# A graph network on one core: attention 1 over fixed tiles of the edge list, 24 of 49 destination blocks dense

## The chip, the cores and the metric

One core of a Trainium2 chip runs the whole program. The metric is the device time of one execution in microseconds; the time before is the median of three runs, 4275.56 us (4267.46 to 4278.62).

The core has engines that run side by side, each its own instructions in order, and that wait for one another by semaphores: PE (matmuls, into the accumulator memory PSUM), DVE (VectorE), ACT (ScalarE), POOL (GpSimd, which here gathers rows by index) and SP (which here issues transfers). DMA queues move data between DRAM and the on-chip memory (SBUF).

## The reference

A graph of 6250 nodes and 200,000 edges, sorted by destination. Two layers of graph attention, then an edge convolution, each behind a layer norm and a relu, each added to x:

```
h = relu(layernorm(x))
x = x + attention2(elu(attention1(h)))        # attention 1: 4 heads of 16; attention 2: 1 head of 128
h = relu(layernorm(x))
x = x + convolution(h, edge attributes)

attention(x):
    feat = x @ W                              # per node
    el, er = sum(feat * attn_l), sum(feat * attn_r)
    e = leaky_relu(el[src] + er[dst], 0.2)    # per edge
    alpha = softmax of e over the edges of each dst
    out[dst] = sum of feat[src] * alpha + bias
```

## The kernel before

Nodes lie in 49 blocks of 128 (the last has 106). The program has four stages.

**Prelude.** x is loaded (`load_x`), normalised, and multiplied by the weights in groups of four blocks (`features`, five steps pipelined by `through`). `write_table` writes a row of 76 floats per node to the DRAM tensor table1: features, logit, and exp(el) and exp(0.2 el). Beside that the sorted edge list is searched: `segments`, `fetch_parts`, `count_parts` and `window_rows` find where each pair of nodes starts (for the counts), `block_segments` and `block_firsts` where each block of 128 nodes starts. Most of these instructions are wrapped in `keep`, which holds an engine's instructions in the written order; the rest is ordered by the framework's scheduler.

**Attention 1** treats its blocks in one of two ways, interleaved in one loop.

*Gathered blocks* (29, in order): a block's edges lie in a window of 34 x 128 = 4352 list entries (CAP), loaded by `load_window` from a start read at run time. Per block, GROUPS cuts the 34 columns in four groups of eight and one of two. For each column `gather` issues one indirect DMA (L346) that fetches 128 table rows by source index into a tile G (six buffers). `attend` then builds a one-hot matrix of the destinations (`ohr`, L351), spreads the destination factors to the edges by matmuls (L387) with the mask `oht` (L377, from a row broadcast to all partitions by `load_low`, L371), takes the larger of the two weights (L389 to L393), multiplies (L394), splits the messages in two halves (L358 on ACT, L359 on DVE), and scatters by one matmul per column (L404) into one accumulator `whole`. At a block's end `sums` are read out (L1038 on ACT, L1039 on DVE), and every four blocks `finish1` ends them.

*Dense blocks* (the last 20, DENSE1): `dense1` works with counts instead of edges: the number of edges between every pair of nodes. One pass treats four destination blocks and two heads and runs over the 49 source blocks seven at a time. It loads the counts `ctc` (L911, 16 transfers of 56 KB each time) and right-hand rows `rc` (L914), builds a steep ramp on ACT (`up`, L942, seven per step), takes its minimum with the counts on DVE (L945), and multiplies on PE (L952, L958). A pass is 16 steps: one that starts it, 14, one that ends it (L965 to L993). Five groups of four blocks and two pairs of heads make ten passes.

*The counts* of all 49 blocks are made in the same loop, in quarters of a block (`cut_windows`, then `count`: one-hots on DVE, L823; matmuls, L834; copies on ACT, L836; a write of 392 KB, L838). Attention 2 reads all of them.

The loop runs over gathered groups. After each, `due` says how many of the 196 counting steps and of the 160 dense steps must have been started: counting ends AFTER = 3 blocks (102 tiles) before the last group, dense steps begin after LAG_D = 3 blocks and end AFTER_D = 20 tiles before the last. `step` delays part of each step by one, so that engines overlap. `fill_rhs1` makes the right-hand rows in the first seven groups.

**Handover.** After the loop the windows of the remaining blocks are loaded too, though no gather reads them, flags are computed, and one run-time test asks whether a general fallback must run (L503). Then the memory of attention 1 is given back.

**Attention 2** runs over pairs of blocks with all counts (`ct`, L1209, eight transfers of 392 KB per pair), the logits spread by L1211 and L1214, ramps on ACT (L1228), minima on DVE (L1232, L1233) and matmuls (L1237). x is loaded again at the second pair. Then the **convolution** over all edges with 1563 gathers.

Memory is handed out by pools; a pool opened after another was closed may lie in its memory, and then waits until that is free. G's pool `gath` of attention 1 is opened after the prelude's pools are closed.

```
GROUPS = ((0, 8), (8, 8), (16, 8), (24, 8), (32, 2))
K = 34
CAP = P * K
AHEAD = 4
DENSE1, LAG_D, AFTER, AFTER_D = 20, 3, 3, 20
```

Of the kernel before, what the change touches and what calls it, by code (L numbers as in the profile page):

```python
# [30 lines left out]
F32 = mybir.dt.float32  # L31
# [13 lines left out]
GROUPS = ((0, 8), (8, 8), (16, 8), (24, 8), (32, 2))  # L45
K = 34
CAP = P * K
# [6 lines left out]
AHEAD = 4  # L54
DENSE1, LAG_D, AFTER, AFTER_D = 20, 3, 3, 20
# [10 lines left out]
def gnn_kernel(ctx: ExitStack, tc: tile.TileContext, x, src, dst, attr4, attr8,  # L66
               W1, al1, ar1, b1, W2, al2, ar2, b2,
               Wl0, Wl1, Ws0, Ws1, Wm1, Wm2, Wtp, Wf0, Wf1, src_t, dst_t, attr4_t, attr8_t, runs,
# [12 lines left out]
    assert NCHUNK * GP * GK == E and E >= CAP and E % (GP * SEG) == 0  # L81
# [13 lines left out]
    NT = src_t.shape[1]  # L95
    NCH = -(-NT // CT)
# [7 lines left out]
    ps_sm = ps_one.enter_context(tc.tile_pool(name="ps_sm", bufs=2, space=PSUM))  # L104
    ps_pre = ExitStack()
# [43 lines left out]
    def load_x():  # L149
        nc.vector.memset(xt[:, FULL, :], 0.0)  # L150
        for b in range(0, FULL, 8):
            n = min(8, FULL - b)
            (nc.scalar, nc.sync)[b // 8 % 2].dma_start(
                xt[:, b:b + n, :], x[b * P:(b + n) * P, :].rearrange("(b p) f -> p b f", p=P))
        nc.scalar.dma_start(xt[:REST, FULL, :], x[FULL * P:, :])
# [5 lines left out]
    pool = one.enter_context(tc.tile_pool(name="att1", bufs=1))  # L161
    seek = ExitStack()
# [6 lines left out]
    nc.sync.dma_start(di[:, :ROWT], rows)  # L169
    nc.sync.dma_start(di[:GP - 1, ROWT:], rows[1:, :1])  # L170
# [8 lines left out]
    w1_sb = const.tile([D, HD], F32, name="w1_sb")  # L179
    nc.scalar.dma_start(w1_sb, W1)  # L180
    a1_sb = const.tile([HD, 2 * H1], F32, name="a1_sb")
    nc.scalar.dma_start(a1_sb, a1_w)
    load_x()

    first_i = const.tile([1, NB], I32, name="first_i")
    over = const.tile([1, NB], F32, name="over")
# [16 lines left out]
    def segments(i0, i1):  # L203
        for i in range(i0, i1):
            below = find.tile([GP, NC * P], BF16, name="belowc", bufs=2)
            keep(nc.vector.tensor_scalar(below, wstarts, df[:, i * WSEG:i * WSEG + 1], None, op0=OP.is_gt))
            for c in range(NC):
                keep(nc.tensor.matmul(pcount[:, c:c + 1], below[:, c * P:(c + 1) * P], ones_b, start=i + c == 0,
                                      stop=i == NSEG - 1 and c == NC - 1))
# [36 lines left out]
    def block_segments():  # L246
        below = find.tile([GP, NB + 1, NS], F32, name="below")
# [12 lines left out]
    def block_firsts():  # L260
# [9 lines left out]
        first = find.tile([1, NB], F32, name="first")  # L270
        keep(nc.vector.tensor_scalar(first, ends[:, :NB], float(E - CAP), None, op0=OP.min))
        keep(nc.vector.tensor_copy(first_i, first))
        keep(nc.vector.tensor_sub(over, ends[:, 1:], first))
        keep(nc.vector.tensor_scalar(over, over, float(CAP), None, op0=OP.is_gt))
        keep(nc.vector.tensor_sub(n_edges, ends[:, 1:], ends[:, :NB]))

    def find_falls():
        falls = find.tile([GP, ROWT], F32, name="falls")
# [6 lines left out]
        keep(nc.vector.tensor_tensor(over, over, falls_at_all, op=OP.max))  # L285

    def low_parts():
        low_i = find.tile([GP, ROWT], I32, name="low_i")
# [7 lines left out]
    def window_start(b):  # L296
        return nc.values_load(
            first_i[0:1, b:b + 1], engines=[SP], min_val=0, max_val=E - CAP,
            skip_runtime_bounds_check_because="first is clamped to this range where it is computed")


    srcw = pool.tile([P, NB, K], I32, name="srcw")
    dstw = pool.tile([P, NB, K], F32, name="dstw")
    raw_dst = {}

    def load_window(b):
        r = window_start(b)
        nc.sync.dma_start(srcw[:, b, :], src[ds(r, CAP)].rearrange("(p k) -> p k", p=P))
        raw_dst[b] = work.tile([P, K], I32, name="dsti", bufs=AHEAD)
        nc.sync.dma_start(raw_dst[b], dst[ds(r, CAP)].rearrange("(p k) -> p k", p=P))  # L310

    def shift_window(b):
        keep(nc.vector.tensor_scalar(dstw[:, b, :], raw_dst.pop(b), -float(b * P), None, op0=OP.add))
# [55 lines left out]
    def load_low(b):  # L369
        t = aw.tile([P, CAP], BF16, name="oht")  # L370
        nc.sync.dma_start(t, dlow[ds(window_start(b), CAP)].partition_broadcast(P))  # L371
        return t

    def node_hot(t):


        nc.vector.tensor_scalar(t, t, own, None, op0=OP.is_equal)  # L377
        return t.rearrange("n (p k) -> n k p", k=K)

# [166 lines left out]
    def rows_of(table, b0, n):  # L546
# [4 lines left out]
    w1t = transposed([w1_sb], HD, nc.vector.tensor_copy)  # L551
    ps = small()
    nc.tensor.matmul(ps[:D, :2 * H1], w1t[:HD, 0, :], a1_sb, start=True, stop=True)
    nc.vector.tensor_copy(ext1[:, :HD], w1_sb)
    nc.vector.tensor_copy(ext1[:, HD:], ps[:D, :2 * H1])
# [17 lines left out]
    slot_k = pool.tile([P, P, 2], BF16, name="slot_k")  # L573
    nc.gpsimd.iota(slot_k, pattern=[[1, P], [0, 2]], base=0, channel_multiplier=0,
                   allow_small_or_imprecise_dtypes=True)
    slot_b = pool.tile([P, P], BF16, name="slot_b")
    nc.gpsimd.iota(slot_b, pattern=[[1, P]], base=0, channel_multiplier=0,
                   allow_small_or_imprecise_dtypes=True)
    pq3 = pool.tile([P, NB, 2 * H1, 3], BF16, name="pq3")
# [16 lines left out]
    def stats(i):  # L596
        b0, n = 8 * i, 8 if i < NB // 8 - 1 else NB - 8 * i
# [3 lines left out]
        c = coefs(b0, n, mv)  # L601
        next(c)
        return c

    co = {}
    w = HD + 2 * H1
# [41 lines left out]
    c0 = stats(0)  # L648
    keep(nc.vector.tensor_copy(df, di))
    deque(c0, 0)  # L650
    c1 = stats(1)
    through(0)
    segments(0, 1)
    through(1)
    deque(c1, 0)
    segments(1, 5)
    c2 = stats(2)
    through(2)
    through(3)
    segments(5, 6)  # L660
    deque(c2, 0)
    segments(6, NSEG)
    window_segments()
    for q in range(2):
        fetch_parts(q)
    c3 = stats(3)
    through(4)
    through(5)
    block_segments()
    deque(c3, 0)  # L670
    c4 = stats(4)
    through(6)
    through(7)
    block_firsts()
    deque(c4, 0)
    c5 = stats(5)
    through(8)
    count_parts(0)
    fetch_parts(2)
    deque(c5, 0)  # L680
    low_parts()
    through(9)
    write_table(0, 24)
    through(10)
    count_parts(1)
    fetch_parts(3)
    through(11)
    through(12)
    count_parts(2)
    fetch_parts(4)  # L690
    through(13)
    write_table(24, 40)
    through(14)
    through(15)
    through(16)
    write_table(40, NB)
    pq = pool.tile([P, NB, 2 * H1], F32, name="pq")
    node_factors(pq, er1, H1)
    split3(pre, pq3, pq, [P, NB, 2 * H1])
    for q in range(3, 5):  # L700
        count_parts(q)
    window_rows()
    sel1 = pool.tile([P, NB, H1], F32, name="sel1")
    nc.vector.tensor_scalar(sel1, t1[:, :, HD:HD + H1], STEEP, None, op0=OP.mult)
    wide1 = widely(pool, t1[:, :, HD:HD + H1])
    find_falls()
# [339 lines left out]

    for b in range(AHEAD):
        load_window(b)
# [563 lines left out]
```

## Time and profile before

| | us |
|---|---|
| median of three runs | 4275.56 |
| the profiled execution | 4266.29 |
| its span, first to last instruction | 4264.5 |
| first to last gather of attention 1 (L346, table1) | 114.4 to 1656.7 |
| first ramp of attention 2 (L1228) | 1707.0 |
| first gather of the convolution | 2289.6 |
| busy over the span: PE, DVE, ACT, POOL | 3058.5, 3570.7, 2829.5, 2703.0 |

A group in the profile names line, engine, operation and tiles, then shapes and how often it ran, its busy time and the mean duration of one in ns, and the idle time of the engine just before with what ended it ("issue" is time in which the engine waited for nothing that the profile shows). A wait line says who waited for whom, the total, how often, and the longest. A timeline line has start, duration, engine, line, operation, tiles, and in brackets the idle time before it and what ended it. Instructions of one engine may overlap a little in the records, so the sum of groups is above the busy time of the engine.

### The profile page before, as it was taken

The page shows a single profiled execution, that of the slowest core. Times are in us where ns is not written, and L with a number is a line of the kernel's source. Part 1 is how long each engine was busy: PE and PEld are TensorE (multiplying, and loading weights), DVE is VectorE, ACT ScalarE, POOL GpSimd, SP SyncE. Part 2 cuts the span into 40 slices and gives each one's busy share as a digit, 9 for nine tenths or more (in the row PEclk, how much of TensorE's full clock was granted, in tenths as well). Part 3 has the DMA queues.
Part 4 walks back from the last instruction along what each step waited for, and adds up shares of the span by engine and source line. Part 5 has one row for each costly group of instructions (what it writes and reads, how often), then busy time and mean ns, then how long its engine had stood idle before and what let it go on. Part 6 is the DMA issues. An engine that isn't in the chain of part 4 may idle for free. (4 is left out here: it accounts for less than half of the span.)

```text
span 4264.5 us, 62159 instructions
## 1 busy us (share of the span) xinstructions
PE 3058.5 (72%) x19331; PEld 2133.9 (50%) x19332; DVE 3570.7 (84%) x6078; ACT 2829.5 (66%) x6395; POOL 2703.0 (63%) x2616
## 2 busy tenths in 40 slices
PE   3365657667767765799996777777777777777777
PEld 3254444444544543688884444444444444444444
DVE  5887868888888875788886999989999998998988
ACT  3456757777777674799995656555555655555655
POOL 3777777777777774100003777777777777777775
PEclk9997868877777776899997888888888888888888
DMA  3555656656666663644441222222222222222221
GB/s 84 163 173 158 171 146 178 174 163 172 184 168 172 170 164 82 248 162 157 166 147 52 62 64 63 62 63 62 64 62 63 62 63 64 62 63 63 63 61 50
DMA packets 413231, 486.83 MB, mean 114 GB/s; under 512 B 251997, under 2 KB 300187, under 8 KB 409165
## 3 DMA queue, kind: packets, MB, share of 16 engines
q1 hardware_dynamic: 293108, 252.64, 20.5%
q0 software_dynamic: 84000, 146.30, 14.4%
q10 hardware_dynamic: 35768, 83.68, 5.2%
q8 instruction: 160, 2.62, 0.3%
q14 instruction: 195, 1.59, 0.1%
HBM read 378.89 MB, written 103.42 MB: 113 GB/s over the span
## 5 line engine op out<-in xcount | busy, mean ns | idle before, releaser
L346 POOL DMA_INDIRECT G<-table,srcc x1563 | 1474.8, 944 | 1003.3 <-DVE kept L1279 527.2
L346 POOL DMA_INDIRECT G<-table,srcw x986 | 1149.5, 1166 | 362.6 <-issue 269.0
L942 ACT ACTIVATE up<-erb,sel 128x512 bf16<-128x512 f32 x980 | 637.0, 723 | 11.8 <-DMA counts<-ca 5.9
L836 ACT CAST ca<-small 128x392 bf16<-128x392 f32 x784 | 350.0, 490 | 239.8 <-PE small L834 221.8
L1373 PE MATMUL whole<-halves,ohr 128*128 128x512 f32 x1563 | 506.8, 463 | 0.7 <-ACT acc L1403 0.7
L1228 ACT ACTIVATE ramp<-erb,sel 128x256 bf16<-128x256 f32 (+1 forms) x1225 | 491.4, 495 | 21.3 <-DVE up L1232 17.4
L1315 ACT ACTIVATE g<-G,a 128x128 f32<-128x128 f32 x1563 | 481.0, 392 | 1.8 <-DMA G<-table,srcc 0.9
L1308 PEld LDWEIGHTS big<-wtp_sb,hid 64*128 64x128 f32 x3126 | 266.1, 251 | 372.4 <-issue 357.5
L958 PE MATMUL up<-up,rc 128*102 128x512 bf16 x980 | 342.7, 507 | 148.6 <-DVE up L945 148.4
L1308 PE MATMUL big<-wtp_sb,hid 64*128 64x128 f32 x3126 | 309.1, 353 | 151.8 <-DVE halves L1362 151.3
L834 PE MATMUL small<-key,lo 128*128 128x98 bf16 x3136 | 295.4, 233 | 129.8 <-ACT ca L836 97.8
L1373 PEld LDWEIGHTS whole<-halves,ohr 128*128 128x128 f32 x1563 | 317.0, 210 | 132.4 <-issue 58.5
L1299 ACT ACTIVATE hid<-layer 128x512 f32<-128x512 f32 x392 | 230.5, 588 | 191.2 <-PE layer L1296 191.2
L1296 PE MATMUL layer<-hid,wm_sb 128*128 128x512 f32 x392 | 342.7, 972 | 12.5 <-ACT hid L1299 11.8
L1296 PE MATMUL layer<-a8t,wm_sb 16*128 16x512 f32 x392 | 230.7, 669 | 153.0 <-ACT hid L1299 141.9
L945 DVE TENSOR_TENSOR up<-up,ctc 128x3584 bf16<-128x3584 bf16 x140 | 282.8, 2021 | 68.2 <-ACT up L942 56.6
L834 PEld LDWEIGHTS <-lo 128*128 128x128 bf16 x3136 | 227.9, 113 | 211.6 <-issue 157.5
L1353 ACT CAST halves<-mess 128x512 fp32r<-128x512 f32 x195 | 114.3, 586 | 329.7 <-DVE mess L1340 329.7
L1345 DVE TENSOR_TENSOR halves<-mess,halves 128x512 fp32r<-128x512 f32 x391 | 267.8, 685 | 60.5 <-ACT halves L1348 43.6
L823 DVE TENSOR_TENSOR lo<-slots,turned 128x2048 bf16<-128x2048 bf16 x196 | 238.6, 1217 | 63.2 <-PE small L834 62.4
L958 PEld LDWEIGHTS <-rc 128*102 128x102 bf16 x980 | 157.9, 165 | 265.3 <-issue 234.4
L1237 PE MATMUL big<-rhs,up 128*128 128x196 bf16 x2401 | 240.6, 250 | 48.2 <-DVE up L1232 38.4
(293 smaller groups left out, 6248.8 us busy)
## 6 DMA issues: line engine op xcount, KB each, us to landing
counts<-ca ACTq DMA_DIRECT2D x196, 392.0 KB
ct<-counts SPq DMA_DIRECT2D x192, 392.0 KB
ctc<-counts SPq DMA_DIRECT2D x1120, 56.0 KB
oht<-dlow SPq DMA_DIRECT2D x29, 1088.0 KB
rc<-rhs SPq DMA_DIRECT2D x70, 358.8 KB
G<-table,srcc POOLq DMA_INDIRECT x1563
G<-table,srcw POOLq DMA_INDIRECT x986
a8t<-attr_rows SPq DMA_DIRECT2D x391, 16.0 KB
```

The costliest lines, as they stand in the source:

```text
L346: nc.gpsimd.indirect_dma_start(out=G[:, c, :], out_offset=None, in_=table, in_offset=bass.IndirectOffsetOnAxis(ap=idx[:, c:c + 1], axis=0))
L834: nc.tensor.matmul(ps[:, k * NKEY:(k + 1) * NKEY], lo[:, a, :, r], ky[:, a, :, r], start=True, stop=True)
L836: nc.scalar.copy(ca[:, :, i * W:(i + WBANK) * W].rearrange("p h (k d) -> p h k d", d=W), ps[:, :WBANK * NKEY].rearrange("p (k h d) -> p h ...
L942: nc.scalar.activation(up[:, i], erb[:, j], AF.Relu, bias=sel1[:, h0 + i, 2 * q + j:2 * q + j + 1], scale=STEEP)
L945: nc.vector.tensor_tensor(by_part, by_part, ct.rearrange("p k a h d -> p h (k a) d"), op=OP.min)
L958: nc.tensor.matmul(sums["ups"][j][:2 * C1, :], r[:, i, c:c + 2 * C1], up[:, i], start=h0 + i == 0, stop=h0 + i == NB - 1)
L1228: nc.scalar.activation(ramp[:, h, :n * P], erb[:, :n * P], AF.Relu, bias=sel2[:, h0 + h, :], scale=STEEP)
L1296: keep(nc.tensor.matmul(ph, w, x[:, :npr * P], start=True, stop=True))
L1308: keep(nc.tensor.matmul(pw[:, c, :], hid[half, j * P:(j + 1) * P], wtp_sb[half].rearrange("x p u -> x (p u)"), start=True, stop=True))
L1315: keep(nc.scalar.activation(g0[:, c], G[:, c, :], AF.Copy, scale=a0[:, c, :]))
L1345: keep(nc.vector.tensor_tensor(ms[:, cs, 1, 1], m, ms[:, cs, 0, 1], op=OP.subtract))
L1373: keep(nc.tensor.matmul(acc, oh[:, c, :], ms[:, c].rearrange("e s h i u -> e (s h i u)"), start=start, stop=stop))
```

## The change

- **Fixed tiles.** The edge list comes in tiles of 128 consecutive edges (`src_t`, `dst_t`, already an input for the convolution); `srcw` and `dstw` are loaded whole. Attention 1 gathers tiles 0 to 807, in stretches of HT = 16 tiles (the first has 8), each centred on 64 nodes. All groups have eight tiles. Nodes are numbered modulo 128 (a ring); a stretch accumulates over the ring, and the sum of a half block is its half of two neighbouring stretches' accumulators. The node factors come in two arrangements, `pq3` and `pqx`, for odd and even stretches. If the list strays too far from its even spread (`find_astray`), the fallback runs. The windows and `load_window`, `shift_window`, `window_start` go.
- **24 dense blocks** instead of 20 (12 passes), 25 gathered. LAG_D and AFTER are now 96 tiles each.
- **Prelude.** x comes in a layout in which a partition's rows are contiguous (`x_t`), its first four blocks ahead of everything else. Statistics go by four blocks; the block search moves behind the table writes. The order on DVE, ACT, PE and SP is the written order. G's pool is opened before the prelude's pools; pools that reuse memory wait for single tiles (`reuse_waits="tile"`) instead of the whole pool.
- **Attention 2's first pair.** When the last counting step is issued, the counting buffers are given back and the counts and logits of the first pair are loaded there, within the loop. Later pairs alternate between two pools of one buffer each, where one pool of two was.

```diff
-GROUPS = ((0, 8), (8, 8), (16, 8), (24, 8), (32, 2))
-K = 34
-CAP = P * K
-AHEAD = 4
-DENSE1, LAG_D, AFTER, AFTER_D = 20, 3, 3, 20
+DENSE1, LAG_D, AFTER, AFTER_D = 24, 96, 96, 20
...
+    NG = NB - DENSE1
+    HALF = P // 2
+    HT = HALF * E // (N * P)
+    NT1 = HT * 2 * NG + HT // 2
...
+    def load_x(parts):
+        for eng, b0, b1 in parts:
+            eng.dma_start(xt[:, b0:b1, :], x_t[:, b0:b1, :])
...
+    gath = one.enter_context(tc.tile_pool(name="gath", bufs=6))
+    srcw = pool.tile([P, NT1], I32, name="srcw")
+    dstw = pool.tile([P, NT1], F32, name="dstw")
...
+    load_x([(nc.sync, 0, 4)])
     nc.scalar.dma_start(w1_sb, W1)
     nc.scalar.dma_start(a1_sb, a1_w)
-    load_x()
+    load_x([(nc.scalar, 4, 8), (nc.sync, 8, 16)])
+    nc.scalar.dma_start(di[:, :ROWT], rows)
+    nc.scalar.dma_start(di[:GP - 1, ROWT:], rows[1:, :1])
+    load_x([(nc.sync, 16, 24), (nc.scalar, 24, 32), (nc.sync, 32, 40), (nc.scalar, 40, NB)])
+    nc.sync.dma_start(srcw, src_t[:, :NT1])
+    nc.sync.dma_start(raw1, dst_t[:, :NT1 + 1])
...
+    def tile_nodes():
+        low = find.tile([P, NT1], I32, name="low1")
+        keep(nc.vector.tensor_scalar(low, raw1[:, :NT1], P - 1, None, op0=OP.bitwise_and))
+        keep(nc.vector.tensor_copy(dstw, low))
...
+    def load_low(c):
+        t0, t1 = max(0, HT * c - HT // 2), HT * c + HT // 2
+        t = aw.tile([P, HT * P], BF16, name="oht", bufs=3)[:, :(t1 - t0) * P]
+        nc.sync.dma_start(t, dlow[t0 * P:t1 * P].partition_broadcast(P))
+        return t
...
+    def node_numbers():
+        node_factors(pq, er1, H1)
+        split3(pre, pq3, pq[:, :NG + 1], [P, NG + 1, 2 * H1])
+        nc.vector.tensor_copy(pqx[:HALF], pq3[:HALF])
+        nc.vector.memset(pqx[HALF:, 0], 0.0)
+        nc.vector.tensor_copy(pqx[HALF:, 1:], pq3[HALF:, :NG])
+        nc.vector.tensor_scalar(sel1, t1[:, :, HD:HD + H1], STEEP, None, op0=OP.mult)
+        return widely(pool, t1[:, :, HD:HD + H1])
...
+    with tc.manual_schedule(engines={nc.vector.engine, nc.scalar.engine, nc.tensor.engine, SP}):
+        slots_up()
+        extend()
+        stats(0)
+        stats(1)
+        ready()
+        through(0)
...
+        low_parts()
+        through(11)
+        tile_nodes()
+        write_table(0, 28)
...
+        write_table(44, NB)
+        w2_sb, a2_sb = load_weights(("w2_sb", W2), ("a2_sb", a2_w))
+        wide1 = node_numbers()
+        count_parts(3)
+        count_parts(4)
+        window_rows()
+        block_segments()
+        find_astray()
+        find_falls()
+        extend2()
+        block_firsts()
...
+    def attending(t0, n, c, oht):
+        first, end_t = max(0, HT * c - HT // 2), HT * c + HT // 2
         G = gath.tile([P, SB, R1], F32, tag="G", name="G")
-        gather(G, table1, srcw[:, b, s:s + n], n)
+        gather(G, table1, srcw[:, t0:t0 + n], n)
...
         def end():
...
+            acc = kept1["acc"]
+            ring = fin.tile([P, HD + H1], F32, name="ring", bufs=2)
+            nc.scalar.copy(ring, acc[:, :HD + H1])
+            nc.vector.tensor_add(ring, ring, acc[:, HD + H1:])
+            if c:
+                b = (c - 1) // 2
+                part = slice(0, HALF) if c % 2 else slice(HALF, P)
+                if c % 2 and b % 4 == 0:
+                    kept1["sums"] = fin.tile([P, 4, HD + H1], F32, name="sums1", bufs=2)
+                nc.vector.tensor_add(kept1["sums"][part, b % 4, :], kept1["ring"][part], ring[part])
+                if c % 2 == 0 and (b % 4 == 3 or b == NG - 1):
+                    finish1(b // 4 * 4, b % 4 + 1, kept1["sums"][:, :b % 4 + 1, :])
+            kept1["ring"] = ring
...
+    def pair_counts(pools, b0, engines):
+        n = min(2, NB - b0)
+        ct = pools[b0 // 2 % 2].tile([P, 2, NQ, NB, QN], BF16, name="ct")
+        for k in range(n):
+            for quarter in range(NQ):
+                engines[k].dma_start(ct[:, k, quarter].rearrange("p h d -> p (h d)"), counts[b0 + k][quarter])
+        return ct
...
+    for g in range(NT1 // SB):
+        t0 = g * SB
+        c = (t0 + HT // 2) // HT
+        if t0 == max(0, HT * c - HT // 2):
+            if c + 2 <= 2 * NG:
+                lows[c + 2] = load_low(c + 2)
+            oht = node_hot(lows.pop(c))
+        step(attending(t0, SB, c, oht))
+        if done == len(steps) and evens is None:
+            building.close()
+            evens = ahead2.enter_context(tc.tile_pool(name="evens", bufs=1, side="right", reuse_waits="tile"))
+            pair0 = pair_counts([evens], 0, [nc.sync] * 2), pair_logits([evens], 0)
+        if g < NB // HS:
+            fill_rhs1(g * HS, HS)
+        due = min(len(steps), len(steps) * (t0 + SB) // (NT1 - AFTER))
...
+        due = min(n_dense, n_dense * (t0 + SB - LAG_D) // (NT1 - LAG_D - AFTER_D))
...
-    for b in range(NG + AHEAD - 1, NB):
-        if b >= NG + AHEAD:
-            load_window(b)
-        shift_window(b)
...
-            ct = dense.tile([P, 2, NQ, NB, QN], BF16, name="ct")
...
+            pools = evens, odds
+            ct, erb = (pair_counts(pools, b0, [nc.sync] * 2), pair_logits(pools, b0)) if b0 else pair0
```

## The prediction

> **What bounds the kernel now.** I read the stretches of the span first, since the shares over the whole span mix stages; then groups, waits and timeline inside attention 1. The chain of waits leads back only to 2342 us, into the edge convolution, which the change leaves alone, so it says nothing here. Columns of the stretches: PE, weight loads, DVE, ACT, POOL busy us (instructions), granted clock, DMA share, GB/s.
>
> ```profile
> 0.00:114.00 114.00, 43.01 (x411) 39.37 (x413) 61.04 (x199) 36.28 (x92) 35.43 (x41) 1.00 0.36 80
> 114.00:1684.00 1570.00, 1015.09 (x7061) 723.75 (x7061) 1263.85 (x2336) 1094.83 (x2160) 1178.46 (x1011) 0.79 0.60 165
> 1684.00:1719.00 35.00, 4.41 (x18) 3.84 (x19) 6.26 (x28) 7.76 (x20) 0.00 (x0) 0.50 0.49 162
> 1800.00:2250.00 450.00, 411.18 (x4364) 371.81 (x4362) 386.70 (x694) 449.45 (x1149) 0.00 (x0) 1.00 0.46 156
> ```
>
> Four things show. A prelude of 114 us in which no engine is busy for more than 61. The attention 1 loop, 1570 us, with DVE fullest by busy time (80%). A handover of 35 us with almost nothing running. Attention 2, full on ACT (449 of 450 us). In the loop the busy share hides the real limit:
>
> ```profile
> L346 POOL DMA_INDIRECT G<-table,srcw x986 | 1149.5, 1166 | 362.6 <-issue 269.0
> DVE lo L823 <- PE small L834: 62.4, 52, 3.3
> DVE w L391 <- DMA G<-table,srcw: 57.5, 14, 9.5
> DVE up L945 <- ACT up L942: 56.6, 44, 4.1
> POOL G L346 <- DVE w L389: 41.4, 15, 10.8
> ```
>
> (First the gather group of the page, then the wait list of 300 to 1640 us.) A gather is 1.166 us and its issue gap 269.0/986 = 0.27, so 986 of them hold POOL for 1418 us; with 25 run fetches (33.8) that is 1452 of the 1543 us between first and last gather, 94%. POOL waits for others under 100 us in all. One stall as the timeline has it:
>
> ```profile
> 597.55 0.94 POOL L346 DMA_INDIRECT G<-table,srcw  x1 [0.30 <-issue]
> 598.80 0.94 POOL L346 DMA_INDIRECT G<-table,srcw  x1 [0.31 <-issue]
> 598.96 0.23 DVE L391 TENSOR_TENSOR w<-w,G 128x64 f32<-128x64 f32 x1 [9.48 <-DMA G<-table,srcw]
> ```
>
> POOL issues gather after gather without a hole, and DVE, with PE and ACT behind it, stands 9.48 us for rows. The loop is held by POOL and DVE together, the gather stream a little ahead.
>
> **The loop, part by part.** Gathers fall from 29 x 34 = 986 to 808. At 1.166 + 0.27 that is -256 us on POOL: 1162 + 34 = 1196 us, so POOL stops being the limit. The rows for a group of eight, and for the dense step:
>
> ```profile
> L351 DVE TENSOR_TENSOR ohr<-slots,dstw 128x1024 fp32r<-128x1024 bf16 x103 | 124.8, 1212 | 3.4 <-PE whole L404 3.3
> L359 DVE TENSOR_TENSOR halves<-msg,halves 128x544 fp32r<-128x544 f32 x103 | 73.8, 716 | 0.4 <-ACT halves L358 0.4
> L394 DVE TENSOR_TENSOR msg<-G,msg 128x512 f32<-128x512 f32 x103 | 70.1, 682 | 0.7
> L389 DVE TENSOR_REDUCE w<-pe 128x64 f32<-128x192 f32 x103 | 35.8, 348 | 10.0 <-PE pe L387 9.8
> L942 ACT ACTIVATE up<-erb,sel 128x512 bf16<-128x512 f32 x980 | 637.0, 723 | 11.8 <-DMA counts<-ca 5.9
> L945 DVE TENSOR_TENSOR up<-up,ctc 128x3584 bf16<-128x3584 bf16 x140 | 282.8, 2021 | 68.2 <-ACT up L942 56.6
> ```
>
> DVE, gathered: with L391 (0.22) and L393 (0.18) a group of eight is 3.36 us; a group of two by the same lines 1.51; a block's node mask (L377) 1.36. Before: 116 x 3.36 + 29 x 1.51 + 29 x 1.36 = 473. After: 101 x 3.36 = 339, 51 masks of half the width at about 0.70 (estimate by width from 1.36 for 4352) = 36, and the ring's adds, two per stretch of sixteen tiles at 0.216 (L1039), 22, for 6 before. Difference -82. The window shifts (L313, 5.5) go: -88. DVE, dense: a pass is 14 x 2.02 plus its end (L977 to L993, 4.9) = 33.2; two more passes +66. Counts (L823, 427), window cutting and the 13 calls of finish1 stay. Net -22: 1264 to 1242.
>
> ACT: a pass is 98 x 0.65 = 63.7 of ramps plus 3.0 of copies, so +133; gathered part -15 x 0.654 - 29 x 0.31 + 22 x 0.22 = -14. Net 1095 to 1214. PE: 178 fewer of 0.08 (L387) and 0.20 (L404) = -50, two passes at 55.7 (L958 343, L952 165, L927 and L974 50, over ten) = +111; 1015 to 1076. So POOL 1196, DVE 1242, ACT 1214, PE 1076: no engine over DVE's present load, and the one that was full is relieved.
>
> What becomes of the idle time: DVE's 306 us fall into 77 behind G (whole loop), 57 behind ACT's ramps, 62 behind PE's counts and small rest. The first goes; the second I let grow by 40, as passes per us rise by a fifth and ACT fills up; ring ends (51 for 29) hold L404 back behind L1039, which cost PE 10.8 us for 29: +8. So 1242 + 306 - 77 + 48 = 1519, on the cautious side, because a gather stall also empties PE and ACT and shows later as other waits (the 8 us waits of L834 and L869 around 600 us are its echo). Bounds: the present idle share stays, 1242/0.805 = 1543 (-27); the loop becomes as full as its first 148 us, where DVE is busy 129.7, 0.876: 1242/0.876 = 1418 (-152). I take **1500, -70**, nearer to the cautious sum.
>
> New loads on SP: 51 mask loads of 512 KB or less for 29 of 1088, 224 count slices of 56 KB more, 98 window loads fewer, and eight loads of 392 KB for attention 2's first pair, put among the count slices about 88 tiles before the end. They may stand at the head of SP's queue until the counting buffers come free, with the slices of the next dense step (L911) behind them, and L945 behind those; a slice wait was 7.2 us in 1340. I cost it at 3, inside the bounds.
>
> The Trainium skill ("DMA: Bandwidth & Descriptors", Specifications) asks for at least 512 B per transfer, below which the engine does a read-modify-write; a count slice is 56 KB over 128 partitions, 448 B, so the rule speaks against more passes. The trace has that queue at 33.5% of 16 engines between 270 and 1655 us with 184,567 packets, 40 ns each; 28,672 more are 72 us per engine, 38 of which the dropped gathers give back, against 40% idle DMA. By the row it costs nothing; were all 72 us exposed as the rule's worst case, the total would be 4212.
>
> **Prelude.** DVE gets the first x at 15.3 us because the edge list is ahead of it in the queue; now a quarter megabyte of x is first, and DVE is held instead by the weight chain of extend, done at 9.9 in the trace. Gathers start at 114.45 when the closing pool lets their buffers go; those buffers now lie outside it, and the index tiles come whole, so only the table is awaited. The order on DVE, ACT, PE and SP is the written one, with three or four groups in flight. DVE's 61 us plus some 5 of added work (seven more coefficient sets, the masked nodes, pqx) from 9.9 on would end at 76 with no hole; at 80% busy, at 92. The block search moves behind the table writes, off the gathers' path but on DVE's, and its fetch (L256) stands in POOL's queue among gathers. The first message work (L389) comes at 128.5 now; I take 95, **-33**; bounds -5 (only the x arrival) and -50.
>
> **Handover.** From 1684 SP loads the last windows, two by two, and all engines stand:
>
> ```profile
> 1684.82 0.90 SPq L310 DMA_DIRECT2D dsti<-in_dst  x1
> ...
> 1702.80 0.33 SPq L310 DMA_DIRECT2D dsti<-in_dst  x1
> 1703.80 1.78 PEld L1211 LDWEIGHTS small<-ident,er 128*128 128x128 f32 x8 [24.23 <-DVEq L503]
> 1716.34 1.09 DVE L1232 TENSOR_TENSOR up<-ramp,ct 128x1792 bf16<-128x1792 bf16 x1 [10.55 <-DMA ct<-counts]
> 1718.74 2.44 PE L1237 MATMUL big<-rhs,up 128*128 128x196 bf16 x14 [9.72 <-DMA rhs<-rhs2d]
> ```
>
> The loads vanish, and the first pair's counts and logits are there already. The same flag test later costs 5.04 us of DVE idle (2289.03). So 1684.2 + 5 + about 6.5 for the first right-hand rows (8.4 from issue to use now, beside 3 MB of counts) = 1696 against 1718.7: **-23**, bounds -12 (only the windows, rows late) and -30. **Attention 2** then reads x in whole rows: ACT stands 3.75 us at 1735 behind its own x loads and is full afterwards: **-4**, 0 to -6. The convolution: 0; it is the same code, and the only thing ahead of it is that attention 2 ends earlier.
>
> **Sum.** -70 - 33 - 23 - 4 = -130. The profiled execution is 4266.3 us (span 4264.5 and 1.8 around it), 9 under the median 4275.6 shown; 4136 for the one, 4146 for the other. I say **4140**.
>
> **Rivals.** (1) The coupling of DVE, ACT and PE, all at about 80%, keeps the idle share: loop -27, total -87, 4185. For it: L945 already waits for L942; against: POOL's holes vanish. (2) The gathers were the only brake: loop -152, total -212, 4060. For it: 94% of POOL; against: 62 us behind PE's counts stay. (3) Slower: ACT takes POOL's place. Between tile 96 and 712 counts and passes run together; 171 of 192 dense steps there ask for 4.17 us of ACT each and the counts for 300, 1.1 ms with the rest by plain addition. If that part has no slack, so that DVE and PE stand behind L942 and the two added passes are serial (133) with nothing won from gathers, then 4276 + 133 - 60 = 4349. It decides from the point where L942 runs without holes while L945's wait exceeds some 200 us; against: ACT idles 475 us in the loop. (4) The new order does not hold in the prelude (POOL or the block search late) and the windows were hidden: only the loop's -70, 4205.
>
> **Chances.** Forecast 0.45 (own range 4095 to 4175), (1) 0.20, (2) 0.18, (3) 0.08, (4) 0.09. The added bounds are -44 and -238, by the median 4232 and 4038; all four are unlikely to meet at one end, so the range 4050 to 4225 leaves out (3) and the outermost of (1) and (2). A difference of 0.3% (13 us) is what this kernel's runs can tell from none: faster 0.89, same 0.03, slower 0.08.
>
> **What would show it.** Right: 808 gathers with POOL occupied under 85% of the loop; DVE's wait behind G under 20 us; DVE about 1240 and ACT about 1215 us busy; first L389 of the loop before 100; the first matmul of attention 2 within 14 us of the loop's last DVE work. Wrong: L945 waiting more than 150 us for L942, a loop above 1545, POOL still back to back, or a prelude above 105.

## The result, and the profile after

| | before | changed |
|---|---|---|
| median, us | 4271.63 (4267.46 to 4278.62, 11 runs) | 4289.06 (4282.06 to 4302.63, 11 runs) |
| ratio | | 1.0043, 95% interval 1.0032 to 1.0053 |
| profiled execution, us | 4266.29 | 4290.12 |
| start to the first w of attention 1 (L389, now L394) | 128.5 | 144.4 |
| from there to the last rr (L879, now L917): the loop | 1555.8 | 1586.9 |
| last rr to attention 2's first matmul | 34.5 | 10.7 |
| attention 2, first to last matmul | 550.5 | 551.0 |
| convolution, first to last gather | 1949.9 | 1950.1 |

The changed kernel is 17 us slower, where 130 us faster was forecast. By stage of the profiled executions, which lie 24 us apart, the start lost 16, the loop lost 31, and the handover won 24. Two groups of the experiments (e5 to e8; f1 to g1) ran on chips on which the kernel before took a quarter longer too (5355 and 5371 us), and they are set against the kernel before on the same chip only.

The stretches of the changed kernel first (columns as in the prediction: PE, weight loads, DVE, ACT, POOL, clock, DMA share, GB/s), then some groups of the page, then DVE's longest waits in the loop:

```profile
0.00:144.00 144.00, 46.42 (x420) 40.07 (x421) 68.91 (x227) 38.91 (x99) 66.76 (x75) 1.00 0.37 92
144.00:1731.00 1587.00, 1051.32 (x7049) 710.36 (x7049) 1265.89 (x2198) 1205.13 (x2345) 934.18 (x801) 0.79 0.61 167
```

```profile
L350 POOL DMA_INDIRECT G<-table,srcw x808 | 938.5, 1162 | 575.2 <-issue 219.1
L980 ACT ACTIVATE up<-erb,sel 128x512 bf16<-128x512 f32 x1176 | 761.0, 723 | 5.8 <-DMA ctc<-counts 2.2
...
L874 ACT CAST ca<-small 128x392 bf16<-128x392 f32 x784 | 348.7, 489 | 195.6 <-PE small L872 174.0
...
L983 DVE TENSOR_TENSOR up<-up,ctc 128x3584 bf16<-128x3584 bf16 x168 | 339.7, 2025 | 100.5 <-ACT up L980 83.2
```

```profile
DVE up L983 <- ACT up L980: 83.2, 69, 2.3
DVE lo L861 <- PE small L872: 60.6, 56, 4.4
DVE oht L382 <- DMA oht<-dlow: 41.0, 17, 6.3
```

POOL is relieved, as forecast: gathers and their issue gaps hold it for 938.5 + 219.1 = 1158 of the 1568 us between the first and the last gather, 74%, and it waits for others 356 us. DVE's 76.7 us behind G are gone from its list. But DVE is busy for the same 80% of a longer loop, and ACT for 76% instead of 70%. The ramps themselves wait for almost nothing (5.8 us in 1176), and DVE's wait for them is no more than 83 us.

The start, in the timeline (start, duration, engine and line, idle time before and what ended it):

```profile
20.87 1.28 ACT L589 ACT_TABLE_LOAD   x1 [20.74 <-DMA xt<-x_tiles]
...
123.54 0.94 POOL L267 DMA_INDIRECT part_i<-in_dst,seg_i  x1 [0.30 <-issue]
125.81 0.18 DVE L273 CAST part<-part_i 50x40 f32<-50x40 int32 x1 [7.48 <-DMA part_i<-in_dst,seg_i]
...
141.05 0.95 POOL L819 DMA_INDIRECT run<-runs,wfirst  x1 [0.30 <-issue]
143.76 0.23 DVE L828 TENSOR_SCALAR hi<-run 128x128 int32<-128x128 int32 x1 [14.45 <-DMA run<-runs,wfirst]
```

DVE has x at 6.2 us, but ACT, which must take the square roots, does nothing before 20.9, and DVE stands 12.5 us for them. ACT's queue issues no transfer from 7.8 to 20.5 us and SP's none from 8.6 to 20.1; what held them is not shown. Later POOL is in a row of gathers from 97.8 on; the two small fetches that DVE needs, part_i and run, stand in that row, though the index of run was ready at 105.4. DVE stands 7.5 + 14.5 = 22 us for them.

The handover:

```profile
1731.04 0.30 DVE L917 TENSOR_TENSOR rr<-x,rr 128x130 bf16<-128x130 f32 x1 [0.36 <-ACT rr L916]
1736.69 1.78 PEld L1106 LDWEIGHTS small<-ident,er 128*128 128x128 f32 x8 [10.03 <-DVEq L508]
...
1742.08 2.45 PE L1291 MATMUL big<-rhs,up 128*128 128x196 bf16 x14 [3.32 <-DVE down L1287]
```

Five microseconds of flag test, then the first pair's ramps and matmuls; no load is waited for. This is what was forecast.

### The profile page after: what moved, and what is told of

Same layout as the page of the kernel before. It is cut to its first block, busy times and chain, and to the rows that moved or that the text cites. A ratio compares the mean times of both kernels' runs of the same rounds, so it can differ in the third digit from the quotient of the medians.

```text
span 4288.3 us, 61875 instructions
## 1 busy us (share of the span) xinstructions
PE 3101.8 (72%) x19325; PEld 2122.6 (49%) x19326; DVE 3580.8 (84%) x5952; ACT 2945.7 (69%) x6586; POOL 2489.4 (58%) x2439
## 5 line engine op out<-in xcount | busy, mean ns | idle before, releaser
L350 POOL DMA_INDIRECT G<-table,srcw x808 | 938.5, 1162 | 575.2 <-issue 219.1
L980 ACT ACTIVATE up<-erb,sel 128x512 bf16<-128x512 f32 x1176 | 761.0, 723 | 5.8 <-DMA ctc<-counts 2.2
L996 PE MATMUL up<-up,rc 128*102 128x512 bf16 x1176 | 388.7, 484 | 161.8 <-DVE up L983 161.3
L1282 ACT ACTIVATE ramp<-erb,sel 128x256 bf16<-128x256 f32 (+1 forms) x1225 | 491.2, 494 | 20.5 <-DVE up L1286 14.0
L874 ACT CAST ca<-small 128x392 bf16<-128x392 f32 x784 | 348.7, 489 | 195.6 <-PE small L872 174.0
L983 DVE TENSOR_TENSOR up<-up,ctc 128x3584 bf16<-128x3584 bf16 x168 | 339.7, 2025 | 100.5 <-ACT up L980 83.2
L872 PE MATMUL small<-key,lo 128*128 128x98 bf16 x3136 | 291.1, 230 | 125.5 <-ACT ca L874 102.2
L1351 PE MATMUL layer<-hid,wm_sb 128*128 128x512 f32 x392 | 346.5, 982 | 15.5 <-ACT hid L1354 14.5
L872 PEld LDWEIGHTS <-lo 128*128 128x128 bf16 x3136 | 224.6, 110 | 217.4 <-issue 166.9
L996 PEld LDWEIGHTS <-rc 128*102 128x102 bf16 x1176 | 182.5, 158 | 300.6 <-issue 256.4
L990 PE MATMUL every<-ctc,rc 128*103 128x512 bf16 x588 | 212.4, 496 | 94.8 <-DMA rc<-rhs 84.3
```

What stands on the lines that cost most here:

```text
L350: nc.gpsimd.indirect_dma_start(out=G[:, c, :], out_offset=None, in_=table, in_offset=bass.IndirectOffsetOnAxis(ap=idx[:, c:c + 1], axis=0))
L872: nc.tensor.matmul(ps[:, k * NKEY:(k + 1) * NKEY], lo[:, a, :, r], ky[:, a, :, r], start=True, stop=True)
L874: nc.scalar.copy(ca[:, :, i * W:(i + WBANK) * W].rearrange("p h (k d) -> p h k d", d=W), ps[:, :WBANK * NKEY].rearrange("p (k h d) -> p h ...
L980: nc.scalar.activation(up[:, i], erb[:, j], AF.Relu, bias=sel1[:, h0 + i, 2 * q + j:2 * q + j + 1], scale=STEEP)
L983: nc.vector.tensor_tensor(by_part, by_part, ct.rearrange("p k a h d -> p h (k a) d"), op=OP.min)
L996: nc.tensor.matmul(sums["ups"][j][:2 * C1, :], r[:, i, c:c + 2 * C1], up[:, i], start=h0 + i == 0, stop=h0 + i == NB - 1)
```

## The experiments

**1. Do the gathers hold the loop?** In each kernel about half the gathers go, and a group without rows of its own works on those of the group before it (shown is the edit of the changed kernel).

```diff
-        G = gath.tile([P, SB, R1], F32, tag="G", name="G")
-        gather(G, table1, srcw[:, t0:t0 + n], n)
+        if t0 // SB % 2 == 0:
+            kept1["G"] = gath.tile([P, SB, R1], F32, tag="G", name="G")
+            gather(kept1["G"], table1, srcw[:, t0:t0 + n], n)
+        G = kept1["G"]
```

> The kernel before, with rows gathered for only three of the five groups of a block (522 gathers instead of 986); the other two groups work on the rows of the group ahead of them, so the sums of the gathered blocks are other ones, and all other work stays. Theory C (the loop is paced by DVE, ACT and PE waiting for one another, and POOL was full only because it followed them): 0 to -45 us against the kernel before, POOL under 60% of the loop and the idle time of DVE found again behind PE and ACT. Theory G (my prediction's reading: the gather stream is a little ahead as the brake): -70 to -150 us, DVE over 85% busy in the loop.

> The changed kernel, with rows gathered for every second group (404 gathers instead of 808); every other group works on the rows of the group ahead of it. Theory C: no more than 15 us faster than the changed kernel, that is 4275 to 4290 us. Theory G in its weak form (even 808 gathers still hold DVE up somewhere): more than 40 us faster, under 4250.

Before: 4188.94 us, ratio 0.9814 (0.9795 to 0.9832), 78 us won; the loop is 1480.5. The changed kernel: 4279.21, ratio 1.0027 (1.0016 to 1.0038), some 10 us under its 4289, or 7 by the two ratios. In e1, with half the gathers of the kernel before, POOL waits for DVE, where DVE waited for POOL (the list of waits, 300 to 1490 us):

```profile
POOL G L346 <- DVE msg L394: 328.2, 23, 29.2
POOL G L346 <- DVE w L389: 143.2, 17, 36.5
```

So the gathers did hold the loop before, as the prediction read it, at 78/464 = 0.17 us each; 808 gathers hold it no more (10/400 = 0.025 each). Theory C in its pure form falls for the kernel before.

**2. Are the four added dense blocks the loss?** One number in the changed kernel, and the same number in the kernel before.

```diff
-DENSE1, LAG_D, AFTER, AFTER_D = 24, 96, 96, 20
+DENSE1, LAG_D, AFTER, AFTER_D = 20, 96, 96, 20
```

> The changed kernel with 20 dense blocks as before: 29 gathered ones, 936 gathers, 160 dense steps. Theory C (a block costs the coupled engines the same either way): 4275 to 4305 us. Theory A (four more dense blocks are the loss, through ACT's ramps and SP's slices): 4250 or less, the loop from the first L394 to the last rr under 1560 us. Theory G: slower, 4320 or more, since 128 gathers come back.

> The kernel before with 24 dense blocks instead of 20: 850 gathers instead of 986, 192 dense steps instead of 160, windows and prelude as they were. If the dense blocks are the loss wherever they stand (20 to 24 cost the changed kernel 82 us): as slow or slower than before, 4265 to 4330. If it is the changed kernel's own arrangement (fixed tiles, dense steps crowded behind tile 96, the early pair): 4200 to 4250, since the gathers that held the loop before are 14% fewer.

With 20 dense blocks the changed kernel takes **4207.43 us, ratio 0.9859 (0.9841 to 0.9876)**: faster than both, by 59 and by 82 us (79 by the ratios), with 128 more gathers. The kernel before with 24 gets slower, ratio 1.0116 (1.0063 to 1.0168), on one of the slower chips. Both say that it is the dense blocks, wherever they stand. The loop with 20:

```profile
146.00:1648.00 1502.00, 976.05 (x6955) 677.07 (x6955) 1248.80 (x2239) 1089.68 (x2163) 1078.98 (x928) 0.80 0.60 171
```

Against the loop with 24 (1587): ACT 115 us less, PE 75 less, DVE only 17 less, POOL 145 more, and 85 us shorter. So the loop's +31 is -53 for everything else in it (1555.8 to 1502.5) and +84 for the four blocks. These two hang on one profile of the changed kernel; a second one (h1, below) has a loop of 1578.1, 9 us less.

**3. Which part of a dense step costs?** Each run leaves out some of one engine's work in the dense steps of the changed kernel: ramps of the second head in three of seven slices of source blocks; the matmuls into the accumulator `every` (L990) beyond the first slice; the counts of three of seven slices; the minima of the second head.

```diff
-                    for i in range(HS):
-                        nc.scalar.activation(up[:, i], erb[:, j], AF.Relu,
-                                             bias=sel1[:, h0 + i, 2 * q + j:2 * q + j + 1], scale=STEEP)
                     by_part = up.rearrange("p h (a d) -> p h a d", d=QN)
-                    nc.vector.tensor_tensor(by_part, by_part, ct.rearrange("p k a h d -> p h (k a) d"), op=OP.min)
+                    if j == 0 or h0 // HS % 2 == 0:
+                        ramp = by_part
+                        for i in range(HS):
+                            nc.scalar.activation(up[:, i], erb[:, j], AF.Relu,
+                                                 bias=sel1[:, h0 + i, 2 * q + j:2 * q + j + 1], scale=STEEP)
+                    nc.vector.tensor_tensor(by_part, ramp, ct.rearrange("p k a h d -> p h (k a) d"), op=OP.min)
```

```diff
-                        for i in range(HS if j == 0 else 0):
+                        for i in range(HS if h0 + j == 0 else 0):
...
-                                             start=h0 + i == 0, stop=h0 + i == NB - 1)
+                                             start=i == 0, stop=i == HS - 1)
```

```diff
-            ct = dn.tile([P, 4, NQ, HS, QN], BF16, name="ctc")
+            even = h0 // HS % 2 == 0
+            if even:
+                kept1["ct"] = dn.tile([P, 4, NQ, HS, QN], BF16, name="ctc")
+            ct = kept1["ct"]
-            for k in range(4):
+            for k in range(4 if even else 0):
```

```diff
-                    nc.vector.tensor_tensor(by_part, by_part, ct.rearrange("p k a h d -> p h (k a) d"), op=OP.min)
+                    if j == 0:
+                        nc.vector.tensor_tensor(by_part, by_part, ct.rearrange("p k a h d -> p h (k a) d"), op=OP.min)
```

First tried on a slower chip:

> The changed kernel with 924 ramps instead of 1176: in three of a pass's seven slices of source blocks the second head takes the minimum of the first head's row instead of a ramp of its own, so its sums are other ones; 252 x 0.647 = 163 us of ACT go, nothing else. Theory A (with 24 dense blocks ACT's ramps pace attention 1): 100 us or more faster than the changed kernel, under 4190. Theory C (no engine alone; DVE, ACT and PE share the loss): 30 to 80 us faster. If another one paces (PE or the slices): under 20 us.

> The changed kernel with 84 instead of 588 matmuls of every (L990), only the first seven source blocks of a pass are summed there; some 180 us of PE go. Theory A: less than 40 us faster than the changed kernel. Theory P (PE, at its granted clock of 0.78 in this loop, is what the dense steps end on): more than 80 us faster, under 4210. Theory C: 30 to 80.

> The changed kernel with the minima (L983) of the first head of a pass only, 84 instead of 168, 170 us of DVE gone; the second head multiplies with its bare ramps. Theory A: less than 40 us faster than the changed kernel. Theory D (DVE, fullest by busy time, paces): more than 100 us faster, under 4190. Theory C: 30 to 80.

> The changed kernel with 768 instead of 1344 count slices (L949): in three of seven steps the counts of the step ahead are used again. Theory S (the slices hold the dense steps: a batch of 16 and its right-hand rows keep SP for some 8 us in the trace, and PE waits 186 us for rc behind them): more than 60 us faster than the changed kernel, PE's wait for rc under 60 us. Theories A and C: 0 to 25 us faster.

e5 0.9861 (0.9803 to 0.9919), e7 1.0104 (1.0038 to 1.0170). In e6 and e8 the degrees no longer matched the number of edges and the fallback ran (218,998 and 67,736 us), so their totals say nothing. Then the ramps again, and the matmuls with the bound of the degree test set out of reach:

> The same kernel as e5_after_fewer_ramps (252 of 1176 ramps left out, 163 us of ACT), once more, since in that call every kernel, the one before too, took a quarter longer. Theory A (ACT is what the four added dense blocks end on): 80 us or more faster than the changed kernel, under 4210. Theory P (PE) or S (the slices): under 20 us. Theory C (shared): 30 to 70 us.

> As e6_after_fewer_matmuls (84 instead of 588 matmuls of L990, some 180 us of PE left out; the degrees come out too small), with the bound of the degree test set so far off that the fallback isn't asked for. Theory P: 80 us or more faster than the changed kernel, under 4210. Theory A: under 20 us. Theory C: 30 to 70.

f1 0.9882 (0.9849 to 0.9915) and f2 0.9871 (0.9827 to 0.9914), on the other slower chip: there, leaving out PE's matmuls won as much as leaving out ACT's ramps. How much either won can't be said without the changed kernel beside them. So the ramps, matmuls and slices once more with the changed kernel itself, on a chip like the first, and the minima on another such chip:

> The changed kernel itself, so that the three below are compared with it on one chip. All theories: 0.2 to 0.8% slower than the kernel before (1.0043 at first), unless this chip takes a quarter longer again, where the ratio is open.

> As f1 (252 of 1176 ramps, 163 us of ACT, left out), now beside the changed kernel. Theory A (ACT is what the added dense blocks end on): 1.9% or more (80 of 4289 us) under h1, and clearly more than h3 and h4. Theory C (a dense step is one chain of slices, ramps, minimum and matmuls, and what shortens any of them helps alike): 0.8 to 1.8% under h1, and h3 and h4 within 0.5% of it.

> As f2 (84 of 588 matmuls of every, some 180 us of PE left out, the degree test out of reach), beside the changed kernel. Theory P (PE paces the dense steps): 1.9% or more under h1, more than h2. Theory A: at most 0.5% under h1. Theory C: 0.8 to 1.8%.

> As e8 (768 of 1344 count slices, the counts of the step ahead used again in three of seven steps), with the degree test out of reach. Theory S (the slices on SP's queue hold the dense steps): 1.5% or more under h1, and PE's wait for rc under a third of h1's. Theories A and P: at most 0.5% under h1. Theory C: 0.8 to 1.8%.

> As e7 (84 of 168 minima, 170 us of DVE, left out of the changed kernel). Theory A (ACT paces; h2 gave 0.74 us for each us of ACT, h3 0.20 for each of PE): at most 40 us under the changed kernel, ratio 0.995 or more. Theory D (DVE, fullest by busy time, paces as well): 100 us or more under it, ratio 0.981 or less.

| left out | median, us | ratio to before | against h1, us | per us of that engine |
|---|---|---|---|---|
| nothing (h1) | 4288.76 | 1.0048 (1.0031 to 1.0066) | | |
| 163 us of ACT's ramps (h2) | 4167.35 | 0.9756 (0.9740 to 0.9772) | -121 | 0.74 |
| some 180 us of PE's every (h3) | 4252.45 | 0.9960 (0.9946 to 0.9974) | -36 | 0.20 |
| 576 count slices (h4) | 4259.96 | 0.9966 (0.9952 to 0.9980) | -29 | 0.05 a slice |
| 170 us of DVE's minima (i2) | 4309.94 | 1.0092 (1.0072 to 1.0111) | +19 by the ratio | below 0 |

ACT's ramps are the largest price, as theory A has it: h2 is 2.8% under h1, where theory A wanted 1.9% or more and clearly more than the others. But ACT doesn't pay alone. h3 is 0.85% under h1 and h4 0.7%, and theory A allowed them 0.5%; PE's matmuls and the slices carry a part.

PE's price in the table is also a low one. In h3 the matmuls that stay take longer (L996 of h1, then of h3):

```profile
L996 PE MATMUL up<-up,rc 128*102 128x512 bf16 x1176 | 385.0, 481 | 157.3 <-DVE up L983 156.3
```

```profile
L996 PE MATMUL up<-up,rc 128*102 128x512 bf16 x1176 | 425.0, 521 | 233.0 <-DVE up L983 221.8
```

Of the 180 us left out, PE's busy time in the loop lost only 87 (1035 to 949), with a granted clock of 0.76 for 0.80. For each us of busy time lost that is 36/87 = 0.41; for ACT, which lost 148 in h2 (1205 to 1057), it is 121/148 = 0.82. In that 121 some of PE is contained: PE was 37 us less busy in h2 (999), with all its matmuls and a clock of 0.82. So ACT costs more than PE here by each way of counting, but on the slower chip, where f1 and f2 came out alike, its lead is not shown.

The prices also make up the four blocks roughly: 115 x 0.74 = 85, PE 75 x 0.20 = 15, 224 slices x 0.05 = 11, less 3 to 22 for 128 gathers by the two prices of experiment 1; that is 89 to 108, an estimate from separate runs, against 82 measured. With 0.41 for PE it would be 105 to 124: prices taken one at a time come to more than the whole.

The dearest engine is idle a quarter of the time. The stretch from 600 to 1400 us shows how the busy times of all engines move from run to run; these are the changed kernel's row and h2's:

```profile
600.00:1400.00 800.00, 539.15 (x3575) 356.79 (x3574) 620.91 (x982) 614.88 (x1193) 441.56 (x376) 0.77 0.60 163
```

```profile
600.00:1400.00 800.00, 565.29 (x3962) 385.65 (x3963) 679.81 (x1098) 592.00 (x1170) 514.27 (x422) 0.80 0.64 181
```

| busy of 800 us | before | changed | e1 | e2 | e3 | h2 | h3 | h4 | i2 |
|---|---|---|---|---|---|---|---|---|---|
| DVE | 659 | 621 | 670 | 627 | 677 | 680 | 645 | 636 | 526 |
| ACT | 604 | 615 | 600 | 616 | 616 | 592 | 640 | 626 | 609 |
| POOL | 605 | 442 | 341 | 226 | 576 | 514 | 474 | 471 | 403 |
| PE | 546 | 539 | 567 | 539 | 544 | 565 | 497 | 540 | 540 |

Whatever is taken away, ACT is busy for 592 to 640 us; DVE goes from 526 to 680 and POOL from 226 to 605. PE is as steady, 539 to 567, but for h3, where its own work was left out. So the shares point at ACT and PE, and only the prices put ACT ahead. In this loop 74 to 80% is as full as ACT gets: 174 us of its idle time in the changed kernel stand ahead of the copies of the counts (L874), behind PE's matmuls (L872). Not told apart is whether the price of a ramp is ACT's time as such or the row of seven ramps, 7 x 0.65 us, that stands ahead of each minimum. And why i2 lost time stays open; it comes with twice the wait of PE for right-hand rows (changed kernel h1, then i2), and its 588 matmuls of every are busy for 234 us, where the two profiles of the changed kernel have 209 and 212. So it is no clean test of DVE's price:

```profile
PE every L990 <- DMA rc<-rhs: 81.1, 38, 6.1
```

```profile
PE every L991 <- DMA rc<-rhs: 158.7, 55, 6.5
```

**4. The start.** The block search goes back between the features, and the first run fetches are held ahead of gathers on POOL; in e4 ahead of all of them.

```diff
         for q in range(2):
             fetch_parts(q)
+        block_segments()
...
     for c in chunks[:2]:
-        fetch_run(c)
+        fetch_run(c, keep)
```

> The changed kernel with the block search back between the features and the two run fetches ahead of the first gather on POOL; no other work changed. Theory Q (in the changed kernel DVE stood 7.5 us for part_i and 14.5 us for run because both fetches stood in POOL's queue among the gathers): first L394 of the loop at 118 to 128 us instead of 144.4, and the whole 15 to 25 us shorter, 4265 to 4275. Rival (the stretch is held by something else that ends just after, the broadcast masks or the first gathers): first L394 after 136, the whole at most 8 us shorter.

4297.08, ratio 1.0077 (1.0058 to 1.0097): nothing won. But the first w came at 122.6 instead of 144.4. The 22 us were lost again between 300 and 356:

```profile
316.23 0.23 DVE L828 TENSOR_SCALAR hi<-run 128x128 int32<-128x128 int32 x1 [8.74 <-DMA run<-runs,wfirst]
...
356.09 0.23 DVE L828 TENSOR_SCALAR hi<-run 128x128 int32<-128x128 int32 x1 [11.44 <-DMA run<-runs,wfirst]
```

There the run fetches stand behind gathers again, and the gathers had begun at 116.0 instead of 97.8; few dense steps have come yet, and I take POOL for the limit there (argued, not tested). Two more attempts, with 20 dense blocks, let eight gathers go first; g1 has the block search early, i1 leaves it late and puts part_i behind the runs (shown is i1):

```diff
         window_rows()
+        gather(rows0, table1, srcw[:, :SB], SB, plain)
+        for c, run in early.items():
+            plain(nc.gpsimd.indirect_dma_start(
+                out=run.rearrange("p j t -> p (j t)"), out_offset=None, in_=runs.rearrange("n j t -> n (j t)"),
+                in_offset=bass.IndirectOffsetOnAxis(ap=wfirst[:, c:c + 1], axis=0)))
         block_segments()
```

> The changed kernel with 20 dense blocks (as e3_after_20_dense, 4207) and the block search and the run fetches ahead of the second group of gathers, with a third run buffer. Theory Q (what e4 won at the start, 22 us, was lost again from 300 to 356 us, because the gathers began 18 us later there and POOL is full up to then): now the gathers start at 98 as in e3, first L394 at 116 to 126, and 8 to 20 us are kept: 4187 to 4200. If the early loop is held by the gathers alone: first L394 early, the whole within 6 us of e3.

> e3_after_20_dense with one change to POOL's queue: after the first eight gathers come the two run fetches and part_i, then the other gathers; the block search stays behind the features, and the first two runs have buffers of their own. Theory Q (the two fetches behind gathers cost the start 22 us, and e4 lost it again because its gathers began 18 us later): gathers begin at 98, first L394 at 118 to 128, the whole 8 to 20 us under e3, ratio to the kernel before 0.981 to 0.984. Rival (up to some 350 us the gathers alone set the pace): first L394 early, ratio 0.985 to 0.987, as e3.

g1 took 0.9826 (0.9794 to 0.9859) of the kernel before on a slower chip, with no e3 beside it, and its gathers began at 106 only. i1 is the fastest of the versions that leave nothing out: **4200.02 us, ratio 0.9832 (0.9819 to 0.9846)**. Its POOL:

```profile
99.67 1.11 POOL L350 DMA_INDIRECT G<-table,srcw  x1 [0.30 <-issue]
...
112.79 0.95 POOL L758 DMA_INDIRECT run<-runs,wfirst  x1 [0.30 <-issue]
...
115.30 0.94 POOL L267 DMA_INDIRECT part_i<-in_dst,seg_i  x1 [0.30 <-DVE off L314]
```

First w at 126.9 for e3's 145.9; of these 19 us the profiled execution keeps 14, the medians 7, the ratios some 11. The interval touches e3's (0.9841 to 0.9876), so this leans to theory Q without settling it.

Not tried: the changed kernel without its early pair, so how much of the handover's 24 us is the pair's and how much the dropped windows' is not known. e3 has that pair too, and its time from the last one-hot of the counts to the last rr is 117 us for 129 before and 137 with 24 blocks; so the longer tail comes with the blocks.

## Why the prediction was wrong, step by step

- **The reading of the bound was right, but only half of it.** POOL's gathers held the loop before (e1), and 808 of them do not (e2). What I didn't see is how close the next limit stood behind POOL, by the prices ACT above all: half of the gathers gone won no more than 78 us.
- **The step that failed is the price of ACT in the loop.** I worked out ACT's new load rightly (1214; measured 1205) and then concluded "no engine over DVE's present load", and of the idle time behind ACT's ramps I wrote "the second I let grow by 40". That compares busy shares of different engines as if each could go to DVE's 80%. ACT's could not here: at 0.74 per us the 115 us that the four blocks bring it cost 85, and with PE and slices 111, where I had let the idle time grow by 40, and by 8 for the ring. The four blocks as a whole cost the loop 84 (e3), and it took 1587 us for the 1500 forecast. The DVE sum on which I based the loop (1242, measured 1266) was near, and the wrong thing to build on as far as i2 shows: 170 us less of DVE's minima won nothing.
- **Rival 3 named the mechanism and missed its sign.** ACT came nearest to taking POOL's place, but I put its deciding point at a wait of L945 for L942 above 200 us; that wait is 83 (now L983 for L980). The pace showed in no wait of the ramps' reader. My signs for the loop (POOL under 85%, no wait behind G, ACT near 1215) came true beside a longer loop, since they tested the relief and not its worth. Two of my signs of being wrong came true: a loop above 1545 and a prelude above 105.
- **The rest of the loop**, fixed tiles and the new arrangement with 20 dense blocks, gave -53 (e3 against the kernel before). Its parts were not told apart, and I had given no figure for it without the four blocks.
- **Prelude, -33 forecast, +16 measured.** The first x did come early, but I let DVE run from 9.9 us on, while ACT stood until 20.9, and named the fetch of the block search, which "stands in POOL's queue among gathers", without pricing it; the run fetches I did not look at. Both fetches cost DVE 22 us. Rival 4 had this for the prelude; its other condition, that the windows were hidden, did not hold. Even cured, the first w comes at 122.6 to 126.9 and not at 95, and the early loop takes the gain back, all of it in e4 and 5 of 19 us in i1.
- **Handover** -23 forecast, -24 measured; **convolution** 0 and 0; **attention 2** -4 forecast, 0 measured.
- **Slices.** I costed 224 more at nothing, with a rule's worst case of 72 us. The rule of the Trainium skill ("DMA: Bandwidth & Descriptors", Specifications) is that transfers under 512 B bring a read-modify-write. By h4 a transfer of 128 rows of 448 B costs 0.05 us, 11 for 224 (estimate): between the two, nearer to nothing. No run shows whether the 448 B are the reason.

The Trainium skill ("Perfetto Trace Analysis", Identifying the Most-Contended Engine) says to take the engine with the highest occupancy as the bottleneck and to optimise it first. By occupancy that is DVE, 80% in this loop; the runs differ, as leaving out 170 us of DVE's minima won nothing and 163 us of ACT's ramps, at 76%, won 121.

## What to carry to other kernels

When work is traded from a full engine to another, don't ask whether the receiving engine has idle time, but how full it ever gets in that loop: one that waits a little at every step can set the pace at 76%. The largest share and the longest wait did not mark it here. A share that stays the same while other engines' work is varied marks the candidates, here ACT and PE; leaving out some of the work of each tells what its time is worth, if one looks at how much busy time really went. And a trade has a best point, so the number that sets it (here 20 or 24 blocks) is tried apart from the rest of the change, which it can hide: the four blocks lost more than all else had won in the loop.

## What the runs showed that was not expected

- Leaving out PE work did not raise the granted clock: 0.77 from 600 to 1400 us in the changed kernel, 0.74 in h3 with 504 matmuls fewer, 0.80 in h2 with all of them and fewer ramps. The same PE group (L996 and its like) took 481, 521 and 458 ns a matmul in h1, h3 and h2.
- A gather costs POOL 1.16 us and an issue gap of 0.3, whatever waits behind it: the run fetch of the changed kernel, 1 KB a row, went out 36 us and 24 gathers after its index was ready.
